# Two packed arrays for the small constants, an earlier load of image 1, and a weight conversion in two halves

## The chip, the cores and the metric

The kernel runs on one core of a Trainium2 chip. The metric is the device time of one launch in microseconds, the median of several runs. The program is one long sequence of instructions on five engines, which are named here as the profile names them: PE multiplies matrices (PEld loads its weights), DVE is the vector engine, ACT the activation engine, POOL the general-purpose engine, SP the engine that issues most of the transfers. [...]

## The reference

Two layers are applied one after the other to x, 32 images of 256 channels by 32 x 32 pixels. Both begin with a group normalisation, and both add their result to their input:

```
x = x + conv(gn(x), weight, bias)      # layer 0
x = x + involution(gn(x), w1, bn, w2, b2)  # layer 1
gn(v):   (v - mean) / sqrt(var + eps) over groups of 8 channels and all pixels
conv:    3 x 3, 256 -> 256 channels; inputs, weights and result rounded to a 16-bit
         float format and clipped at 65504
involution: y = relu(batchnorm(w1 @ v)); k = w2 @ y + b2, a 7 x 7 kernel for each
         pixel and each of 16 groups of channels; out = that kernel on v around the pixel
```

The constants of layer 1 besides w2 and b2 are the four vectors of the batch norm and w1; layer 0 has its weights and its bias.

## The kernel before, in words

**Stages.** One step n of the main loop (line 552) issues a small slice of the work of up to three images at once. `front` (line 289) is a generator that issues the first half of an image's work in slices: sums (add_up, line 221), mean (243), sums of squares (247), variance (252), 1/sqrt (259), scale and offset (263), the normalised input xq (apply, line 283), the convolution (line 337) in four units of 18 matmuls, of which nine use the first half of the weights and nine the second. For each unit DVE clips the result (line 351) and adds it with the bias to x (line 353), and ACT adds x up for layer 1 (line 224). Then come layer 1's normalisation into xn, the product with w1 (line 385), and transposes (line 400). The per-pixel kernels (line 415), their move to memory (`scatter`, line 469), their reload as bands (`load_bands`, line 482) and the involution's matmuls (`sums`, line 504) follow later in the loop. Each image takes 16 steps; image 1 enters `front` 16 steps after image 0.

**Order.** Everything inside `with tc.manual_schedule()` (line 550) keeps the order in which it is written on each engine. What stands ahead of it, lines 126 to 201, is placed between these instructions by the planner of the framework, as its own estimate of when inputs arrive suggests. The chain of small instructions from the batch norm's constants (lines 182 to 188) is such a case: on DVE it was put behind line 353 of image 0's first unit, and between the instructions of the second.

**Group normalisation.** `group` (line 228) takes per-partition sums, transposes them on DVE, adds eight of them, and transposes back. It is called for the mean and again for the variance, so each normalisation goes ACT, DVE, ACT, DVE, ACT several times.

**The start.** SP issues the two halves of image 0, the two halves of the convolution's weights (line 161, into the space of the later bands), w2 in two pieces (165), b2 in fourteen (170), the bias (173), w1 (175), the four vectors of the batch norm in two pieces each (180), and three writes of zeros to the borders of the memory for the per-pixel kernels (201). Behind these stand the loads of images 1 to 3, which the loop asks for at line 591, 63 steps ahead of an image's involution (LOAD). `quantize_weights` (line 203) clips and converts the weights to 16 bits on DVE, both halves one after the other, at step FRONT + 2: in DVE's queue that is after image 0's mean and ahead of its variance. POOL then fills the two bands and the ring w_sb with zeros.

Of the kernel before, what the change touches and what calls it, by code (L numbers as in the profile page):

```python
# [9 lines left out]
F32 = mybir.dt.float32  # L10
AF = mybir.ActivationFunctionType
ALU = mybir.AluOpType

P = 128
# [4 lines left out]
CH = C // P  # L19
K0, PAD0 = 3, 1  # L20
K1, PAD1 = 7, 3
TAPS = K1 * K1
CR = 64
G = 16
# [5 lines left out]
F16_MAX = 65504.0  # L30
# [21 lines left out]
V = 2  # L52
A = G // V
# [3 lines left out]
SW = K1 * G  # L57
S = H + 2 * PAD1
T = 4
TW = P // T  # L60
# [6 lines left out]
NPIX = 6  # L67
RING = 32
SCRATCH = 4096
FRONT = -56  # L70
LOAD = -63
LEAD = 18
# [3 lines left out]
def tile_quant_conv_then_involution(  # L76
# [1 line left out]
    tc: tile.TileContext,  # L78
    x: bass.AP,
    w0: bass.AP,  # L80
    bias0: bass.AP,
    w1: bass.AP,
    bn_gamma: bass.AP,
    bn_beta: bass.AP,
    bn_mean: bass.AP,
    bn_var: bass.AP,
    w2: bass.AP,
    b2: bass.AP,
    out: bass.AP,
):  # L90

# [1 line left out]
    nc = tc.nc  # L93
    PSUM = bass.MemoryType.PSUM

    const = ctx.enter_context(tc.tile_pool(name="const", bufs=1))
# [9 lines left out]
    def load_x(b):  # L106
        xt = xpool.tile([P, CH, N], F32, tag="x", name=f"x_{b}")
        for h in range(CH):
            nc.sync.dma_start(xt[:, h], x[b, h * P : (h + 1) * P])
        return xt  # L110
# [15 lines left out]
    x_tiles = {0: load_x(0)}  # L126
# [18 lines left out]
    bands = [const.tile([P, SIDES, WINC * WB + PAD], F32, name=f"band_{i}") for i in range(NBAND)]  # L145
# [7 lines left out]
    w_sb = const.tile([P, 2, RING, A, WIN, V], F32, name="w_sb")  # L153
# [3 lines left out]
    wq = const.tile([P, CH, K0 * K0, C], F16, name="wq")  # L157
    staged = []
    for kh in range(CH):
        wf = bands[kh].rearrange("p d n -> p (d n)")[:, : K0 * K0 * C].rearrange("p (k c) -> p k c", c=C)  # L160
        nc.sync.dma_start(wf, w0[kh * P : (kh + 1) * P])
        staged.append(wf)
    w2_sb = const.tile([P, K1, SW], F32, name="w2_sb")
    for i in range(2):
        nc.sync.dma_start(w2_sb[i * CR : (i + 1) * CR], w2)
    b2_sb = const.tile([P, 2, 2, SW], F32, name="b2_sb")
    for dj in range(K1):
        t, e = divmod(dj, 2)
        for r in range(2):
            nc.sync.dma_start(b2_sb[t * TW : (t + 1) * TW, e, r], b2[dj].partition_broadcast(TW))  # L170

    bias_sb = const.tile([P, CH], F32, name="bias_sb")
    nc.sync.dma_start(bias_sb, bias0.rearrange("(h p) -> p h", p=P))
    w1_sb = const.tile([P, CH, CR], F32, name="w1_sb")
    nc.sync.dma_start(w1_sb, w1.rearrange("(h p) o -> p h o", p=P))

    bn = const.tile([P, 4], F32, name="bn")
    for i, v in enumerate((bn_gamma, bn_beta, bn_mean, bn_var)):
        for r in range(2):
            nc.sync.dma_start(bn[r * CR : (r + 1) * CR, i : i + 1], v.unsqueeze(1))  # L180
    bn_ve = const.tile([P, 1], F32, name="bn_ve")
    nc.vector.tensor_scalar(bn_ve, bn[:, 3:4], BN_EPS, None, ALU.add)  # L182
    bn_r = rsqrt(bn_ve, [P, 1], "bn")
# [16 lines left out]
        )  # L200
        nc.sync.dma_start(to, bands[NBAND - 1][:H, 0, :n].unsqueeze(1).to_broadcast([H, cols, n]))

    def quantize_weights():

        for kh in range(CH):
            nc.vector.tensor_scalar(wq[:, kh], staged[kh], F16_MAX, -F16_MAX, ALU.min, ALU.max)
            nc.gpsimd.memset(bands[kh], 0.0)
        nc.gpsimd.memset(w_sb, 0.0)

    class GroupNorm:  # L210

# [195 lines left out]
    def weights(b, r0):  # L407

        pws = [ps_w.tile([P, 2, 2, SW], F32, tag=f"pw{i}", name=f"pw{i}") for i in range(2)]
        for r in range(2):  # L410
            for t in range(T):
                for i in range(2):
                    half = slice(i * CR, (i + 1) * CR)
                    dj = slice(2 * t, min(2 * t + 2, K1))
                    nc.tensor.matmul(  # L415
                        pws[i][t * TW : (t + 1) * TW, : dj.stop - dj.start, r],
                        y_sb[b % 2][half, (r0 // 2 + r) * W : (r0 // 2 + r + 1) * W],
                        w2_sb[half, dj],
                        start=True,
                        stop=True,  # L420
                    )
        for i in range(2):
            for e in range(2):
                p = P if e == 0 else (K1 // 2) * TW
                for r, rows, d0, d1, at in ring_pieces(b, r0 + 2 * i):
                    evict(pws[i][:p, e, r : r + rows], e, r, rows, d0, d1, at)
# [42 lines left out]
    def scatter(b, k, part):  # L469

        at = (b * H + k * TR) % RING
        for dj in range(part, K1, 2):
            t, e = divmod(dj, 2)
            to = bass.AP(
                tensor=wd.tensor,
                offset=wd.offset + k * TR * ROW + dj * WPIX + (K1 - 1 - dj) * WB,
                ap=[[WPIX, TW], [ROW, TR], [1, WB]],
            )
            rows = w_sb[t * TW : (t + 1) * TW, e, at : at + TR]
            nc.sync.dma_start(to, rows.rearrange("p s a r v -> p s (a r v)"))  # L480
# [23 lines left out]
    def sums(b, m):  # L504

        k, d = divmod(m, SIDES)
        j0 = 0 if d else PAD1
        band = bands[(b * K + k) % NBAND][:, d]
        px = pixels[(b * K + k) % NPIX][:, d]
        for h in range(CH):  # L510
            for v in range(2):
                for g, at, top, f, l in windows(b, m):
                    p = slice(g * KP, (g + 1) * KP)
                    of = band[p, V * g * XR + j0 * WB : V * g * XR + (j0 + WINI) * WB]
                    of = of.rearrange("p (j a r v) -> p j a r v", a=A, r=WIN, v=V)
                    for t in range(T):
                        a = h * T + t
                        nc.tensor.matmul(  # L518
                            at[t * TW : (t + 1) * TW, h, :, f - top : l - top],
                            px[p, a, v * GC : v * GC + TW],  # L520
                            of[:, :, a, f - top : l - top, v],
                            start=(h, v) == (0, 0),
                            stop=(h, v) == (CH - 1, 1),
                        )

    def add_windows(b, m):

        d = m % SIDES
        to = x_tiles[b].rearrange("p h (r c) -> p h r c", c=W)
        j0 = d * (JC - PAD1)  # L530
        for g, at, top, f, l in windows(b, m):
            x_at = to[:, :, f:l, j0 : j0 + WINI]
            of = at.rearrange("p h j r -> p h r j")[:, :, f - top : l - top]
            nc.vector.tensor_tensor(x_at, of, x_at, ALU.add)  # L534

    def store(b, k):

        cols = slice(k * NT, (k + 1) * NT)
        nc.sync.dma_start(out[b].rearrange("(h p) n -> p h n", p=P)[:, :, cols], x_tiles[b][:, :, cols])
# [5 lines left out]
    def due(n, lag):  # L545

        b, i = divmod(n - lag, per)
        return (b, i) if 0 <= b < B else (None, None)

    with tc.manual_schedule():  # L550
        fronts = {}
        for n in range(FRONT, B * per + 2):
            b, i = due(n, FRONT)
            if i == 0:
                fronts[b] = front(b)
            later = list(fronts)
            for part in range(2):
                for b in list(later):
                    got = next(fronts[b], fronts)
                    if got is fronts:  # L560
                        fronts.pop(b)
                    if got is not LATER:
                        later.remove(b)
            if n == FRONT + CH:
                quantize_weights()
            b, i = due(n, 0)
            if b is not None and i % 2 == 0:
                sums(b, i // 2)
            b, i = due(n, 1)
            if b is not None and i % 2 == 0:  # L570
                add_windows(b, i // 2)
                if i // 2 == M - 1:
                    store(b, 1)
                    x_tiles.pop(b)

            b, i = due(n, 2)
            if b is not None and i == 2 * (M - 1 - SIDES):
                store(b, 0)
            b, i = due(n, -LEAD)
            if b is not None and i % 2 == 0:  # L580
                weights(b, i // 2 * WR)

            for part in range(2):
                b, i = due(n, -LEAD + 1 + part)
                if b is not None and i % 2 == 0:
                    for k in range(K):
                        if i // 2 == min((k + 1) * TR // WR, H // WR - 1):
                            scatter(b, k, part)
            b, i = due(n, LOAD)
            if i == 0 and b > 0:  # L590
                x_tiles[b] = load_x(b)

            b, i = due(n, 3 - 4 * NBAND)
            if b is not None and i % 4 == 0:
                load_bands(b, i // 4)
# [37 lines left out]
```

## Time and profile before

| | |
|---|---|
| median of three runs | 1375.84 us |
| the three runs | 1378.53, 1371.69, 1375.84 us |
| the profiled execution | 1370.77 us, of which its span is 1368.9 us |
| busy share of the span | PE 92%, POOL 74%, DVE 60%, ACT 53% |
| mean granted clock of PE | 0.988 |
| first matmul of image 0's convolution | 18.06 us after the start |
| first matmul of image 1's convolution | 40.63 us |
| first matmul of the involution (line 518) | 93.62 us |

A line of the timeline has the start in microseconds, the duration, the engine, the line of the kernel, the operation, the tile written and the tile read, shape and count; in brackets stands how long the engine had been idle and what ended it. Adjacent instructions of one kind are put together, so that the duration of such a line can contain waits. An SPq line tells of SP's queue: the time it takes to issue a transfer, not that of the transfer. A row of the table of windows has the stretch, its length, the busy time of an engine with the number of instructions, the granted clock of PE (1.00 is full speed), the busy share of the transfer engines, and the rate.

### The profile page before, as it was taken

The numbers are of one execution on the slowest core, as the hardware profiler recorded it, in microseconds if no ns is written. First come the engines' busy times: TensorE is split into PE (matmuls) and PEld (weight loads), VectorE is DVE, ScalarE is ACT, GpSimd is POOL, SyncE is SP. The second block draws the span as 40 slices with busy tenths as digits, with TensorE's granted clock in tenths as the row PEclk, the third lists the DMA queues.
The fourth block names the chain that finished last, engine by engine and source line by source line (L and its number), as shares of the span: only waits on it lengthen the run. The fifth ranks groups of instructions, "written<-read, shape, count | busy, mean of one in ns | idle before, by whom it ended". The sixth has DMA issues, their size and how long they took to land.

```text
span 1368.9 us, 69378 instructions
## 1 busy us (share of the span) xinstructions
PE 1261.3 (92%) x29440; PEld 805.5 (59%) x29440; DVE 820.2 (60%) x2539; ACT 726.8 (53%) x1699; POOL 1012.1 (74%) x1818
## 2 busy tenths in 40 slices
PE   4799999999999999999999999999999999999664
PEld 2356666656665665666666566556656656666543
DVE  3366566666666666665666666656666666666542
ACT  4866565465655555665555565545555555553300
POOL 9057777778777777877777777777777777778875
PEclk9999999999999999999999999999999999999997
DMA  6089999999999999999999999999999999999995
GB/s 218 6 221 289 278 283 290 296 274 287 277 285 284 279 287 282 291 290 282 289 286 285 276 279 282 280 294 269 282 290 278 286 285 287 289 287 268 275 273 170
DMA packets 366563, 369.93 MB, mean 270 GB/s; under 512 B 78960, under 2 KB 308528, under 8 KB 366000
## 3 DMA queue, kind: packets, MB, share of 16 engines
q1 hardware_dynamic: 280240, 235.90, 58.0%
q0 software_dynamic: 86016, 129.60, 34.1%
q8 instruction: 234, 3.83, 1.2%
q14 instruction: 73, 0.60, 0.1%
HBM read 184.43 MB, written 180.76 MB: 267 GB/s over the span
## 4 chain that ended last, share of the span: by engine, by line
PE 72%; DMA 13%; issue 4%; POOL 3%; ACT 3%; SPq 2%; DVE 2%; POOLq 0%; DVEq 0%; ACTq 0%
PE pc L337 29%; PE acc L518 23%; PE pw L415 13%; DMA band<-wd 7%; PE py L385 4%; DMA wd<-w_sb 4%; PE pt L400 3%; POOL band L493 3%; ACT junk L224 1%; SPq L480 1%; DMA x<-in_x 1%; DMA out<-x 1%; DVE w_sb L439 1%; DMA w_sb<-in_w 1%; SPq L493 0%
## 5 line engine op out<-in xcount | busy, mean ns | idle before, releaser
L493 POOL DMA_DIRECT2D band<-wd x1792 | 978.0, 548 | 343.2 <-DMA band<-wd 209.9
L439 DVE TENSOR_TENSOR w_sb<-pw,b_sb 128x224 f32<-128x224 f32 (+7 forms) x1280 | 331.4, 324 | 434.7 <-PE pw L415 428.7
L337 PE MATMUL pc<-xq,wq 128*128 128x496 f16 (+3 forms) x2304 | 534.5, 378 | 30.6 <-ACT xq L283 24.3
L518 PE MATMUL acc<-band,pixels 64*32 64x190 f32 (+1 forms) x16384 | 428.5, 329 | 50.5 <-DMA band<-wd 28.0
L337 PEld LDWEIGHTS <-wq 128*128 128x128 f16 x2304 | 206.5, 98 | 324.3 <-issue 110.9
L518 PEld LDWEIGHTS acc<-band,pixels 64*32 64x32 f32 x16384 | 300.8, 106 | 141.8 <-issue 89.4
L415 PE MATMUL pw<-w_sb,y 64*32 64x224 f32 (+1 forms) x8192 | 290.6, 330 | 17.7 <-issue 16.8
L534 DVE TENSOR_TENSOR x<-acc,x 128x380 f32<-128x380 f32 (+1 forms) x512 | 262.3, 512 | 32.9 <-PE acc L518 24.0
L415 PEld LDWEIGHTS pw<-w_sb,y 64*32 64x32 f32 x8192 | 186.1, 105 | 48.3 <-issue 33.4
L404 ACT COPY pixels<-pt 128x512 f32<-128x512 f32 x128 | 73.7, 576 | 237.2 <-PE pt L400 237.2
L224 ACT ACTIVATE junk<-x 128x512 f16<-128x512 f32 (+1 forms) x192 | 146.4, 763 | 16.6 <-DVE bn_ve L182 6.0
L224 ACT ACTIVATE junk<-x,mean 128x1024 f16<-128x1024 f32 x128 | 147.1, 1149 | 4.3
L255 ACT ACTIVATE s<-back,eps 128x2 f32<-128x2 f32 x64 | 19.0, 296 | 198.6 <-DVE back L240 198.5
L351 DVE TENSOR_SCALAR q<-pc 128x512 f16<-128x512 f32 x128 | 87.1, 680 | 18.2 <-PE pc L337 18.1
L283 ACT ACTIVATE xn<-x,off,rstd 128x512 f32<-128x512 f32 x128 | 96.2, 800 | 0.0
L353 DVE SCALAR_TENSOR_TENSOR x<-q,bias_sb,x 128x512 f32<-128x512 f16 x128 | 94.6, 739 | 0.3
L400 PEld LDWEIGHTS pt<-ident,xn 128*128 128x128 f32 x512 | 63.3, 141 | 26.6 <-issue 2.7
L400 PE MATMUL pt<-ident,xn 128*128 128x128 f32 x512 | 77.3, 274 | 0.8 <-ACT pixels L404 0.7
L283 ACT ACTIVATE xq<-x,off,rstd 128x1024 f16<-128x1024 f32 x64 | 75.8, 1227 | 1.0 <-PE pc L337 0.9
L385 PEld LDWEIGHTS py<-xn,w_sb 128*64 128x64 f32 x2048 | 62.8, 138 | 16.8 <-issue 6.7
L385 PE MATMUL py<-xn,w_sb 128*64 128x64 f32 x2048 | 67.7, 224 | 2.8 <-ACT xn L283 2.2
L245 ACT ACTIVATE mean<-back 128x2 f32<-128x2 f32 x64 | 12.6, 196 | 101.2 <-DVE back L240 101.2
(40 smaller groups left out, 372.7 us busy)
## 6 DMA issues: line engine op xcount, KB each, us to landing
wd<-w_sb SPq DMA_DIRECT2D x896, 160.0 KB
band<-wd POOLq DMA_DIRECT2D x1792, 70.5 KB, 4.9
x<-in_x SPq DMA_DIRECT2D x64, 512.0 KB
out<-x SPq DMA_DIRECT2D x64, 512.0 KB
band<-wd SPq DMA_DIRECT2D x256, 70.5 KB
band<-in_w SPq DMA_DIRECT2D x2, 1152.0 KB
w_sb<-in_w SPq DMA_DIRECT2D x2, 196.0 KB
wd<-band SPq DMA_DIRECT2D x2, 180.0 KB
```

The lines of the kernel that those rows point to most:

```text
L224: nc.scalar.activation(junk[:, n0:n1], src[:, h, n0:n1], func, bias=bias, accum_out=self.sums[:, i : i + 1])
L283: nc.scalar.activation(dst, src, AF.Identity, bias=self.off[:, one], scale=self.rstd[:, one])
L337: nc.tensor.matmul(pc.rearrange("p (r c) -> p r c", c=W)[:, r0 - nt * RT : r1 - nt * RT, c0:c1], wq[:, kh, k, mh * P : (mh + 1) * P], xq[: ...
L351: nc.vector.tensor_scalar(q, pc, F16_MAX, -F16_MAX, ALU.min, ALU.max)
L353: nc.vector.scalar_tensor_tensor(xt[:, mh, cols], q, bias_sb[:, mh : mh + 1], xt[:, mh, cols], ALU.add, ALU.add)
L385: nc.tensor.matmul(py[i * CR : (i + 1) * CR, cols], w1_sb[:, kh, :], px[:, r : r + 2], start=kh == 0, stop=kh == CH - 1,)
L400: nc.tensor.transpose(pt[:, i, h * P : (h + 1) * P], xn[:, h, (m + i) * P : (m + i + 1) * P], ident)
L415: nc.tensor.matmul(pws[i][t * TW : (t + 1) * TW, : dj.stop - dj.start, r], y_sb[b % 2][half, (r0 // 2 + r) * W : (r0 // 2 + r + 1) * W], w ...
L439: nc.vector.tensor_tensor(to, of[:, :, d0:d1], bias[:, :, d0:d1], ALU.add)
L493: queue.dma_start(band[j::JC, :, j * WB : j * WB + WPIX], src)
L518: nc.tensor.matmul(at[t * TW : (t + 1) * TW, h, :, f - top : l - top], px[p, a, v * GC : v * GC + TW], of[:, :, a, f - top : l - top, v], ...
L534: nc.vector.tensor_tensor(x_at, of, x_at, ALU.add)
```

## The change

The host packs the bias, the four vectors of the batch norm and w1 into one array of 128 rows (`early`, 134 numbers a row) and w2 and b2, already repeated as the tiles need them, into another (`late`, 1232 numbers a row). The kernel loads each in one transfer and takes the tiles as views. The load of image 1 is asked for between the two; the loop loads images from 2 on. `quantize_weights` does one half of the weights a call: the first at step FRONT + 2 as before, the second four steps later, which puts it behind image 0's variance and reciprocal in DVE's queue.

```diff
+EARLY = CH + 4 + CH * CR
+LATE = K1 * SW + 2 * 2 * SW
...
-    w2_sb = const.tile([P, K1, SW], F32, name="w2_sb")
-    for i in range(2):
-        nc.sync.dma_start(w2_sb[i * CR : (i + 1) * CR], w2)
-    b2_sb = const.tile([P, 2, 2, SW], F32, name="b2_sb")
-    for dj in range(K1):
-        t, e = divmod(dj, 2)
-        for r in range(2):
-            nc.sync.dma_start(b2_sb[t * TW : (t + 1) * TW, e, r], b2[dj].partition_broadcast(TW))
-
-    bias_sb = const.tile([P, CH], F32, name="bias_sb")
-    nc.sync.dma_start(bias_sb, bias0.rearrange("(h p) -> p h", p=P))
-    w1_sb = const.tile([P, CH, CR], F32, name="w1_sb")
-    nc.sync.dma_start(w1_sb, w1.rearrange("(h p) o -> p h o", p=P))
-
-    bn = const.tile([P, 4], F32, name="bn")
-    for i, v in enumerate((bn_gamma, bn_beta, bn_mean, bn_var)):
-        for r in range(2):
-            nc.sync.dma_start(bn[r * CR : (r + 1) * CR, i : i + 1], v.unsqueeze(1))
+    early_sb = const.tile([P, EARLY], F32, name="early_sb")
+    nc.sync.dma_start(early_sb, early)
+    bias_sb = early_sb[:, :CH]
+    bn = early_sb[:, CH : CH + 4]
+    w1_sb = early_sb[:, CH + 4 :].rearrange("p (h o) -> p h o", h=CH)
+    x_tiles[1] = load_x(1)
+    late_sb = const.tile([P, LATE], F32, name="late_sb")
+    nc.sync.dma_start(late_sb, late)
+    w2_sb = late_sb[:, : K1 * SW].rearrange("p (k n) -> p k n", n=SW)
+    b2_sb = late_sb[:, K1 * SW :].rearrange("p (e r n) -> p e r n", r=2, n=SW)
...
-    def quantize_weights():
-
-        for kh in range(CH):
-            nc.vector.tensor_scalar(wq[:, kh], staged[kh], F16_MAX, -F16_MAX, ALU.min, ALU.max)
-            nc.gpsimd.memset(bands[kh], 0.0)
-        nc.gpsimd.memset(w_sb, 0.0)
+    def quantize_weights(kh):
+
+        nc.vector.tensor_scalar(wq[:, kh], staged[kh], F16_MAX, -F16_MAX, ALU.min, ALU.max)
+        nc.gpsimd.memset(bands[kh], 0.0)
+        if kh == CH - 1:
+            nc.gpsimd.memset(w_sb, 0.0)
...
-            if n == FRONT + CH:
-                quantize_weights()
+            if n in (FRONT + CH, FRONT + CH + 4):
+                quantize_weights((n - FRONT - CH) // 4)
...
-            if i == 0 and b > 0:
+            if i == 0 and b > 1:
                 x_tiles[b] = load_x(b)
```

## The prediction

> **What bounds the kernel now.** I read the page first, then the chain of waits up to 90 us, then the timelines of DVE, PE and SP from 0 to 60 us, and last the table of windows for PE's clock.
>
> ```profile
> PE 1261.3 (92%) x29440; PEld 805.5 (59%) x29440; DVE 820.2 (60%) x2539; ACT 726.8 (53%) x1699; POOL 1012.1 (74%) x1818
> PE   4799999999999999999999999999999999999664
> ```
>
> PE is the bound of the body: 90% or more in all slices but the first two and the last three. The diff touches only what runs in the first 35 us, so all there is to win lies in the first slices (34 us each), in the time in which PE is idle or slow. Three places are left: PE starts at 18.06, it idles from 34.87 to 40.63, and after that it runs at half speed.
>
> ```profile
> 11.71 1.81 DVE L206 TENSOR_SCALAR wq<-band 128x2304 f16<-128x2304 f32 x1 [1.44 <-DMA band<-in_w]
> 13.45 0.19 DVE L234 STREAM_TRANSPOSE across<-sums 128x32 f32<-128x32 f32 x1
> 14.14 0.29 ACT L255 ACTIVATE s<-back,eps 128x2 f32<-128x2 f32 x1 [3.58 <-DVE back L240]
> 18.06 16.80 PE L337 MATMUL pc<-xq,wq 128*128 128x512 f16 x72 [18.06 <-ACT xq L283]
> 24.53 3.65 SPq L109 DMA_DIRECT2D x<-in_x  x6
> 24.93 0.15 DVE L182 TENSOR_SCALAR bn_ve<-bn 128x1 f32<-128x1 f32 x1
> 29.43 1.06 ACT L224 ACTIVATE junk<-x 128x1024 f16<-128x1024 f32 x1 [3.51 <-DMA x<-in_x]
> 36.25 0.30 ACT L255 ACTIVATE s<-back,eps 128x2 f32<-128x2 f32 x1 [0.82 <-DVE back L240]
> 39.35 2.36 ACT L283 ACTIVATE xq<-x,off,rstd 128x1024 f16<-128x1024 f32 x2
> 40.63 6.03 PE L337 MATMUL pc<-xq,wq 128*128 128x512 f16 x18 [5.76 <-ACT xq L283]
> 47.44 3.97 PE L337 MATMUL pc<-xq,wq 128*128 128x512 f16 x18 [0.78 <-DVE q L351]
> ```
>
> Image 0's variance (13.45) stands behind the second weight conversion, which waits for its transfer; ACT had nothing to do for 3.58 us. Image 1's load is issued at 24.53, its data land at 29.35, and ACT waits 3.51 us for them.
>
> ```profile
> 37.50:38.00 0.50, 0.00 (x0) 1.00 0.00 0
> 38.00:38.50 0.50, 0.00 (x0) 0.51 0.00 0
> 44.50:45.00 0.50, 0.50 (x3) 0.67 0.00 0
> 45.00:46.00 1.00, 1.00 (x6) 1.00 0.00 0
> ```
>
> The clock (the number after the count) falls to half at 38.0 and is back at 44.83. So the 18 matmuls at 40.63 take 6.03 us where those at 47.44 take 3.97.
>
> [...] 38.0 to 44.83 is two times 3.41, and the falls and rises after 1300 us (1311.2, 1314.6, 1324.8, 1328.2) lie on the same grid. It goes further: a 2.58 us gap (1307.21 to 1309.79) was enough to halve the clock and one of 2.23 (1290.44 to 1292.67) was not; by the grid, a window falls when PE was busy for less than about 41% of it, that is idle for over 2.0 us. [...] of the weights' 256 packets the last falls between 10 and 11 us and most of w2 comes after them, but the first piece of b2 slipped ahead.
>
> **The change, part by part.**
>
> *Transfers.* 26 small transfers leave SP's queue, which spends 2.60 to 22.45 on them (6.6 of that waiting for earlier ones), and two come in at about 0.45 each. Image 1's pair is issued at about 3 to 4 instead of 24.53. In ring order it lands behind x of image 0, the weights and `early`: the second weights' landing (11.65) plus 1.12 MB at 0.43 MB/us, 14.3. If all that SP issues after it (`late` 0.63 MB, images 2 and 3 2.1 MB) shares the engines evenly, 6.3 later, 20.6. ACT needs it at 23.0 (below), so it is hidden either way. The border writes now meet POOL's fill of the third band, over at 7.7; images 2 and 3 may wait behind that, and are first read at 51.9, so nothing. `late` (w2) lands by 21 at the worst and is first used at 60.9 before. POOL's fills keep their rate: the first two bands 14.15 to 26.04 behind its fill of pixels, later than both conversions in either kernel; the ring until 34.6, first written after 61. Nothing.
>
> *Second conversion moved.* Its 1.8 us leave the path. The squares of image 0 end on ACT at 10.57, the first conversion at 10.28, so the variance begins at 10.62 instead of 13.45: **2.83** earlier. With what follows unchanged (13.45 to 18.06 is 4.61) PE starts at 15.23. The second conversion goes behind the reciprocal (11.8), where its data are in (11.65): 11.85 to 13.65. PE needs that half after nine cold matmuls of 0.43, at 19.1; DVE is free until 20.6. If image 1 and `late` shared the transfer engines with it, it would land 1.75 MB / 0.43 = 4.1 later and end at 17.6: still covered. The first half has no cover: each microsecond that it lands after 8.5 costs one beyond the first 0.3. Nothing new is ahead of it; I take 0, and 1.0 as the upper end.
>
> *Batch norm's chain.* It has ten small instructions, nine on DVE at 0.14 to 0.16 and a root on ACT. Its place is chosen by the planner, and the trace of before can't show the new one. Behind the second conversion it is free (DVE idles from 13.65 to 20.6). Ahead of the variance DVE waits for `early`, which lands at about 11.65 + 0.2: 1.2 us of the 2.83 go. One of them between variance and reciprocal costs 0.2. Below nothing is excluded: DVE was not late behind it before. I take 0, with 1.2 as the end.
>
> *Image 1 no longer late.* Image 0's first unit is added up on ACT until 23.0 (25.84 - 2.83), image 1's sums take 2.39 and end at 25.4, the mean follows the second unit at 26.7, and the squares end at 29.5. What is late next? DVE's queue holds image 1's variance behind the third unit of image 0. PE finishes that at 31.07 - 2.83 = 28.24 (the units take 3.81 each, the last ends at 34.87). From the end of a unit to line 255 it took 2.14 (46.66 to 48.80), from line 255 to line 283 3.10 (36.25 to 39.35), from there to the matmul 1.28. So image 1's convolution starts at 28.24 + 6.52 = 34.76 and not 40.63: **5.87** earlier, of which 2.83 is the earlier start and 3.04 the smaller gap: PE ends image 0 at 32.04 and idles 2.72 instead of 5.76.
>
> *Clock.* Before lost 6.03 - 3.97 = 2.06. A gap of 2.72 escapes only if a grid boundary splits it into two parts under 2.0 each: (2.0 - 0.72) / 3.41 = 37%. Otherwise the clock is low for one window of 3.41, 0 to 0.7 of it in the gap, which costs 1.4 to 1.7. I take 1.65, a gain of 0.4; the other end is 2.06.
>
> *Sum.* 5.87 + 0.4 = 6.3; less 0.1 for the small instructions of the batch norm that may stand on the path, **6.2**. After 46 us the waits are all relative (ACT and PE alternate on the chain up to 90 us, PE alone after), so this stays. From the profiled 1370.77 (span 1368.9 and 1.87 around it) that gives 1364.6. This execution is 5.1 below the median of the runs; the four executions known (1370.77, 1371.69, 1375.84, 1378.53) average 1374.2 and lie within 7.8. I start from the 1374.2: **1368.0**.
>
> **The rivals.**
> - *The clock stays up.* 2.06 in place of 0.4: 7.9, so 1366.3. For it: two more gaps of about 2 us that it survived; against it: the 2.58.
> - *The batch norm's chain goes ahead of the variance.* 5.0: 1369.2. For it: the planner puts it where it thinks that its data are in, and these now come third. Against it: before, it stood where the real data landed, so the planner's idea of landings isn't far off.
> - *It goes ahead of image 0's mean: slower.* DVE would stand from 7.0 until `early` lands at L, with the mean, squares and variance behind it. PE then starts at L + 0.2 + 8.2 (18.06 - 2.83 - 7.04) and image 1's convolution at L + 27.9; with the 0.4 of clock it is slower from L = 13.1. In ring order L is 11.8 (1.3 faster); if `early` shares the engines with image 1 and `late` it is 15.7: 2.6 slower, 1376.8. For it: b2's first piece shows that order can be broken; but that let a small one go first.
> - *The gain is given back.* The transfer engines are 92% busy over the span (58.0 and 34.1), and a stage that they pace could take the 6 us. Then 1373.5. Against it: up to 180 us no wait for a transfer stands on PE's chain; waits for bands appear from 1290 on.
>
> **How the numbers follow.** Likeliest 0.42, clock up 0.20, chain ahead of the variance 0.22, ahead of the mean 0.08, given back 0.08. A median of a few runs with a spread of 7.8 blurs each by about 3. The first three with that reach from 1363 to 1372; the other two, 0.16, lie beyond 1373. Range 1363.0 to 1374.5. About 0.5% (6.9 us) is what a measurement of this kernel can tell from no change; from the median of the runs that bound is 1369.0. Below it fall about 60% of the likeliest case, 75% of the second and 45% of the third: faster 0.50; same 0.45; slower 0.05, from the spread alone, as no case reaches +6.9.
>
> **What would show it.** First matmul at 15.2, image 1's at 34.8 and its first 18 matmuls in 4.0 or 5.6; the second conversion behind line 261; ACT not waiting for image 1; the batch norm's chain between 13 and 21 on DVE. The start wrong: line 234 at 12 or later behind line 182 or 206. The sum wrong: image 1's convolution 6 earlier and the involution's first matmul (93.62) not earlier by as much.

## The result, and the profile after

Over twelve runs each, the changed kernel takes 1371.58 us in the median (1363.8 to 1378.67) and the kernel before 1380.26 (1371.69 to 1388.19). The ratio is 0.9935 with a 95% interval of 0.9909 to 0.9961: 9.0 us faster, between 5.4 and 12.6. The kernel before had 1375.84 in its first three runs; its later ones were slower. The profiled execution of the changed kernel took 1367.45 us, its span is 1365.7.

The page's first part and its slices, after. PE's share is the same. Besides slices at the two ends, one digit differs from before: an 8 for a 9 in the 34th slice.

```profile
PE 1262.2 (92%) x29440; PEld 808.8 (59%) x29440; DVE 819.5 (60%) x2539; ACT 725.7 (53%) x1699; POOL 1012.0 (74%) x1818
PE   4999999999999999999999999999999998999675
```

The timeline of the start, after. Lines are numbered anew: 194 is the weight conversion, 171 the batch norm's first instruction, 244 the variance on ACT, 272 the normalised input, 326 the convolution.

```profile
3.35 0.97 SPq L105 DMA_DIRECT2D x<-in_x  x2
10.72 0.21 DVE L223 STREAM_TRANSPOSE across<-sums 128x32 f32<-128x32 f32 x1 [0.44 <-ACT junk L213]
11.44 0.30 ACT L244 ACTIVATE s<-back,eps 128x2 f32<-128x2 f32 x1 [0.82 <-DVE back L229]
11.85 1.68 DVE L194 TENSOR_SCALAR wq<-band 128x2304 f16<-128x2304 f32 x1
13.45 0.14 DVE L171 TENSOR_SCALAR bn_ve<-early_sb 128x1 f32<-128x1 f32 x1
15.35 16.72 PE L326 MATMUL pc<-xq,wq 128*128 128x512 f16 x72 [15.35 <-ACT xq L272]
23.06 1.06 ACT L213 ACTIVATE junk<-x 128x1024 f16<-128x1024 f32 x1
30.40 0.30 ACT L244 ACTIVATE s<-back,eps 128x2 f32<-128x2 f32 x1 [0.86 <-DVE back L229]
33.51 2.35 ACT L272 ACTIVATE xq<-x,off,rstd 128x1024 f16<-128x1024 f32 x2
34.78 5.66 PE L326 MATMUL pc<-xq,wq 128*128 128x512 f16 x18 [2.71 <-ACT xq L272]
41.22 3.97 PE L326 MATMUL pc<-xq,wq 128*128 128x512 f16 x18 [0.78 <-DVE q L340]
```

The variance stands right behind the squares (10.72, where it was 13.45), the second conversion behind it with its data already there (no wait in brackets), and ACT goes on to image 1 at 23.06 without waiting. PE's gap ahead of image 1 is 2.71 us where it was 5.76.

PE's clock around that gap, after (stretch, length, busy time and count, clock, transfers):

```profile
34.50:35.00 0.50, 0.22 (x2) 1.00 0.04 16
35.00:35.50 0.50, 0.50 (x3) 0.63 0.00 0
38.00:38.50 0.50, 0.50 (x2) 0.50 0.00 0
38.50:39.00 0.50, 0.50 (x4) 0.96 0.00 0
```

It falls at 35.13 and is back at 38.54, one stretch of 3.41 us; the first 18 matmuls take 5.66 and not 3.97. In this trace and in that of before, every later change of the granted clock lies a whole number of steps of 3.41 us behind the first rise (18.06 after, 20.94 before): the fall at 35.13 is five steps behind it, and that at 38.01 in the kernel before is five, too. Such a step is what the prediction calls a window of the grid.

The involution's first matmul comes at 87.41 (93.62 before), 6.21 earlier. Behind it the lead wanders. Read at ACT's activation of each image (line 392 before, 381 after) it is 6.22 for image 0, 3.3 for image 6, 0.7 for image 19, 6.2 for image 25, slightly below nothing for images 26 and 28 (-0.1 and -0.6) and 1.3 for image 31. From image 3 to image 30 an image takes 38 to 43 us in either trace, and once 44.6. So one pair of profiles can't say what is left at the end, and the experiments are read in two ways: the start from the trace, where the order is fixed, and the whole from the ratios over many runs.

### The profile page after: what moved, and what is told of

It reads as the page before. It is cut to its first block, busy times and chain, and to the rows that moved or that the text cites. A ratio compares the mean times of both kernels' runs of the same rounds, so it can differ in the third digit from the quotient of the medians.

```text
span 1365.7 us, 69351 instructions
## 1 busy us (share of the span) xinstructions
PE 1262.2 (92%) x29440; PEld 808.8 (59%) x29440; DVE 819.5 (60%) x2539; ACT 725.7 (53%) x1699; POOL 1012.0 (74%) x1818
## 4 chain that ended last, share of the span: by engine, by line
PE 67%; DMA 19%; issue 4%; POOL 4%; ACT 3%; DVE 2%; SPq 1%; POOLq 0%; DVEq 0%; ACTq 0%
PE pc L326 27%; PE acc L507 21%; DMA band<-wd 14%; PE pw L404 12%; DMA wd<-w_sb 5%; POOL band L482 4%; PE py L374 3%; PE pt L389 3%; ACT junk L213 1%; DVE w_sb L428 1%; SPq L469 1%; ACT xn L272 0%; DMA x<-in_x 0%; SPq L482 0%; ACT xq L272 0%
## 5 line engine op out<-in xcount | busy, mean ns | idle before, releaser
L428 DVE TENSOR_TENSOR w_sb<-pw,late_sb 128x224 f32<-128x224 f32 (+7 forms) x1280 | 331.0, 324 | 437.7 <-PE pw L404 437.6
L404 PE MATMUL pw<-late_sb,y 64*32 64x224 f32 (+1 forms) x8192 | 288.0, 331 | 18.7 <-issue 17.8
L404 PEld LDWEIGHTS pw<-late_sb,y 64*32 64x32 f32 x8192 | 186.2, 106 | 46.7 <-issue 31.9
L213 ACT ACTIVATE junk<-x 128x512 f16<-128x512 f32 (+1 forms) x192 | 146.3, 762 | 14.4 <-DVE x L342 11.9
L342 DVE SCALAR_TENSOR_TENSOR x<-q,early_sb,x 128x512 f32<-128x512 f16 x128 | 94.8, 740 | 0.3
L374 PEld LDWEIGHTS py<-xn,early_sb 128*64 128x64 f32 x2048 | 62.6, 138 | 17.0 <-ACT mean L234 8.1
L374 PE MATMUL py<-xn,early_sb 128*64 128x64 f32 x2048 | 67.5, 224 | 3.1 <-ACT xn L272 2.2
```

The costliest lines, as they stand in the source:

```text
L213: nc.scalar.activation(junk[:, n0:n1], src[:, h, n0:n1], func, bias=bias, accum_out=self.sums[:, i : i + 1])
L342: nc.vector.scalar_tensor_tensor(xt[:, mh, cols], q, bias_sb[:, mh : mh + 1], xt[:, mh, cols], ALU.add, ALU.add)
L374: nc.tensor.matmul(py[i * CR : (i + 1) * CR, cols], w1_sb[:, kh, :], px[:, r : r + 2], start=kh == 0, stop=kh == CH - 1,)
L404: nc.tensor.matmul(pws[i][t * TW : (t + 1) * TW, : dj.stop - dj.start, r], y_sb[b % 2][half, (r0 // 2 + r) * W : (r0 // 2 + r + 1) * W], w ...
L428: nc.vector.tensor_tensor(to, of[:, :, d0:d1], bias[:, :, d0:d1], ALU.add)
```

## The experiments

In this table the start is the involution's first matmul, and the gain at the start is against 93.62. The gain in all is worked out from the ratio, times the median of the kernel before in the same set of runs. Each start is that of one profiled execution.

| kernel | first matmul | image 1's convolution | involution | gain at the start | ratio, 95% interval | gain in all |
|---|---|---|---|---|---|---|
| before | 18.06 | 40.63 | 93.62 | | | |
| changed | 15.35 | 34.78 | 87.41 | 6.2 | 0.9935, 0.9909 to 0.9961 | 9.0 |
| e1 split only | 15.50 | 41.43 | 94.23 | -0.6 | 1.0012, 0.9989 to 1.0035 | -1.7 |
| e2 image 1 third | 18.09 | 37.95 | 90.58 | 3.0 | 0.9963, 0.9937 to 0.9989 | 5.1 |
| e3 packed only | 18.87 | 39.70 | 90.67 | 2.9 | 0.9928, 0.9903 to 0.9953 | 9.9 |
| e4 all but the load | 15.65 | 35.26 | 87.89 | 5.7 | 0.9897, 0.9864 to 0.9930 | 14.2 |
| e5 before, fills later | 18.06 | 40.58 | 93.54 | 0.1 | 1.0001, 0.9976 to 1.0026 | -0.1 |
| e6 changed again | 15.20 | 35.71 | 86.68 | 6.9 | 0.9937, 0.9904 to 0.9969 | 8.7 |
| e7 unpacked | 15.22 | 35.70 | 88.32 | 5.3 | 0.9939, 0.9912 to 0.9965 | 8.4 |
| e8 pulled | 15.23 | 32.2 | 83.99 | 9.6 | 0.9888, 0.9849 to 0.9928 | 15.5 |
| e9 fill first | 15.31 | 36.07 | 87.14 | 6.5 | one run, 1362.45 us | |
| e10 batch norm ahead | 22.74 | 43.28 | 94.25 | -0.6 | one run, 1379.82 us | |
| e11 pulled, warmed | 15.69 | 31.1 | 82.89 | 10.7 | 0.9846, 0.9815 to 0.9878 | 21.3 |
| e12 pulled again | 15.50 | 33.5 | 85.28 | 8.3 | 0.9854, 0.9830 to 0.9879 | 20.2 |

Where image 1's convolution follows without a gap (e8, e11, e12) its start is worked out: the end of the run of 90 matmuls less the 3.97 us of the last 18. The ratios of e1 to e4 are of one set of runs, those of e5 to e8 of a second (medians of the kernel before 1378.27 and 1383.12), those of e11 and e12 of a third (1382.93).

**The conversion alone.**

```diff
-    def quantize_weights():
+    def quantize_weights(kh):
...
-            if n == FRONT + CH:
-                quantize_weights()
+            if n in (FRONT + CH, FRONT + CH + 4):
+                quantize_weights((n - FRONT - CH) // 4)
```

> The kernel before with the weight conversion in two halves and nothing else. My theory, that the gains of the parts are limited by image 1's load: the first matmul at 15.3 us instead of 18.06, but image 1's data still land at 29.35, so that its convolution starts at 40.6 as before, with a gap of 8.5 us on PE instead of 5.76, and the involution's first matmul stays at 93.6, within 0.5. Time as before, ratio 1.000 within 0.003. Rival, that the parts add up: image 1's convolution at 37.8, the involution at 90.8, 2.8 us faster.

The first matmul came 2.6 us earlier, and nothing of it reached image 1. The parts don't add up: alone, this one is worth nothing. But the second conversion went otherwise than I had thought, and image 1's convolution was 0.8 later than before and not level. The timeline of this run, DVE, POOL, PE and ACT:

```profile
13.33 6.81 DVE L205 TENSOR_SCALAR wq<-band 128x2304 f16<-128x2304 f32 x1 [1.25 <-DMA band<-in_w]
12.95 5.97 POOL L206 MEMSET band<- 128x7056 f32 x1
20.20 15.75 PE L337 MATMUL pc<-xq,wq 128*128 128x496 f16 x63 [0.78 <-DVE wq L205]
30.00 0.20 ACT L115 ACTIVATE bn_s<-bn_ve 128x1 f32<-128x1 f32 x1 [3.46 <-DVE bn_ve L182]
30.24 1.06 ACT L224 ACTIVATE junk<-x 128x1024 f16<-128x1024 f32 x1
```

The second conversion took 6.81 us in place of 1.8, beside POOL's fill of the first band (5.97 us), which had begun 0.38 earlier. Its nine cold matmuls done, PE waited 0.78 us for it. Runs e5 and e9 take this up.

Whether this wait is also what made image 1 late is not shown. ACT begins image 1's sums at 30.24, where it began them at 29.43 before, and two things come at that time. On ACT the root of the batch norm's chain stands ahead of the sums at 30.00; in this kernel the chain was put behind image 0's second unit, which PE's wait delays. And SP issued image 1's load at 25.40, 0.87 later than before, as the fourteen pieces of b2 took it 13.48 us and not 12.62; landing as long after its issue as before (29.35 less 24.53), the data would be there at 30.2, an estimate.

**Image 1's load alone.** `x_tiles[1] = load_x(1)` goes ahead of the load of w2, and nothing else changes.

> The kernel before with image 1's load moved ahead of all small constants; those stay in their 26 transfers, and the weights are converted in one go. My theory: first matmul at 18.06 as before, ACT does not wait for image 1, the gap ahead of its convolution is 2.7 us, the convolution starts at 37.6 instead of 40.63, the involution at 90.2 with the 0.4 us of clock: 3.4 us faster, ratio 0.9975. Rival, that the small constants, now 0.9 us later, hold up the first unit's addition: the bias is read at 24.27 before, and all that follows moves by what it is late.

Image 1's convolution moved by 2.7 and the involution by 3.0; 3.4 was expected. The gap was 2.93, all of it in one step of 3.41 us counted from the first rise, and the clock fell at the step's end (38.30). The constants' lateness cost little: the bias, issued at 20.01, was there for line 354 at 24.42 (24.27 before).

**The packing alone.** The two arrays and transfers as in the change, image 1's load left to the loop, the conversion in one go.

> The small constants in two arrays and transfers, image 1's load left to the loop, the weights converted in one go. My theory: SP is free of the 26 issues, so that image 1's load goes out by 13 us at the latest and its data are there well ahead of 25.9, when ACT can use them. So it gives what the third place gives: image 1's convolution at 37.6, the involution at 90.2, ratio 0.9975. Rival, that the place of the load matters: its data come behind the border writes and images 2 and 3 and ACT waits for them; then image 1's convolution is later than 37.6 by that wait.

The involution moved by 2.9 where 3.4 was foreseen, and that it came so near is luck. Image 1's convolution was due at 37.6 and came at 39.70: the first matmul was 0.8 later than before, since the first conversion took 4.48 us beside POOL's fills of the pixels, and the 72 matmuls took 18.13 us with a long cold start. The clock stayed up after the gap, which gave most of that back. The gap itself is as foreseen, 2.71. Image 1's load goes out at 3.62 (first half) and 11.9, and ACT never waits for it. The third place closes the gap as freeing SP's queue does (2.93 in e2). The ratio, 0.9928, says more than the start does: 9.9 us (6.5 to 13.4).

**All but the load's place.** The changed kernel, with image 1's load left to the loop.

> The changed kernel with image 1's load left to the loop (two packed transfers and the conversion in halves stay). My theory: ACT first needs image 1 at 23.06 and finds it there; first matmul 15.35, image 1's convolution 34.8, involution 87.4, all as in the changed kernel; ratio to before as there, 0.9935 within its interval. Rival, that the third place is needed once the first matmul is earlier: ACT waits for image 1 after 23.06, and image 1's convolution is later than 34.8 by that wait.

The start is that of the changed kernel but for 0.5 (the first matmul 0.3 later). The gap is 2.71, as in the changed kernel, and ACT does not wait for image 1. So the load's third place is worth nothing at the start once the constants are packed. The ratio, 0.9897, came out below the expected interval's edge; again more over the whole than at the start.

**POOL's fills out of the way, in the kernel before.** Both fills of bands behind both conversions.

> The kernel before, but POOL fills both bands with zeros only behind both weight conversions, where it filled the first between them. New theory, from the second conversion that took 6.81 us beside POOL's first band fill when only the conversion was split: DVE's conversion and a POOL fill exclude each other, and in executions in which the second weights land after 13 us the kernel before loses up to 6 us to that fill. Then this one shows a second conversion of at most 1.9 us, a first matmul near 18 to 19, and over many executions it is faster than the kernel before by 1 to 3 us, ratio 0.998 to 0.999. Rival: the 6.81 us were waiting for data, and this kernel is as before, 1.000.

No difference is seen. In the profiled execution the second conversion came at 11.82 and took 1.71, ahead of both fills that were moved (14.15, as in the kernel before). So this profile is no test of the theory, and nothing speaks for a frequent loss in the kernel before; the interval, which reaches down to 0.9976, doesn't exclude the 1 to 3 us that were expected. That a fill keeps a conversion out stayed open until e9.

**The changed kernel again.**

> The changed kernel once more, beside the others of this job, for a second profile of its start and a ratio on the same chip. First matmul within 15.2 to 15.7, image 1's convolution within 34.7 to 35.3, ratio 0.9935 within its interval of 0.9909 to 0.9961.

The first matmul is where it should be and the gap is again 2.71, but the clock went otherwise. The timeline of PE in this run:

```profile
15.20 17.81 PE L326 MATMUL pc<-xq,wq 128*128 128x512 f16 x72 [15.20 <-ACT xq L272]
35.71 3.97 PE L326 MATMUL pc<-xq,wq 128*128 128x512 f16 x18 [2.71 <-ACT xq L272]
```

Image 0's 72 matmuls took 1.1 longer, being cold for longer: the first rise of the clock in the trace is at 20.12 and not at 18.06. Up to that rise the column of the clock reads 1.00, and the cold start shows in the pace alone, 0.43 us a matmul where 0.22 is usual later. Image 1's first 18 ran at full speed (5.66 in the other profile). Image 1's convolution is at 35.71, outside the 34.7 to 35.3 that I gave, for that reason.

**The start without the packing.** The bias, then image 1's load, ahead of the other small constants, which stay in 25 transfers; the conversion in halves; fills of bands behind both.

> The changed kernel's start without its packing: image 1's load behind the bias, ahead of the other small constants, which stay in their many transfers; the conversion in halves; POOL fills the bands behind both halves, so that it can't stand in DVE's way. Theory, that only the start matters: first matmul 15.3, image 1's convolution 34.8 to 35.3, involution 87.4 to 88, and the ratio to before is that of the changed kernel in this job within 0.003. Rival, that the packed constants are worth something in the body too (the two kernels with them gained 7 to 8 us more over the whole time than at the start, the two without them nothing clear): the same start, but a ratio higher than the changed kernel's by 0.004.

First matmul and gap are nearly the changed kernel's (15.22, 2.80). Image 1's convolution (35.70) and the involution (88.32) came later than I gave, since the cold start was long (72 matmuls in 17.69) and the clock fell as well. The ratios in one set of runs, 0.9939 and 0.9937, are the same. This speaks for a gain of the start alone. The intervals still allow some 4 us either way.

**Image 1's normalisation earlier.**

```diff
+PULL = 7
...
         gn.finish()
+        if b == 1:
+            yield from stages(PULL)
...
-            if i == 0:
+            if i == 0 and b != 1:
                 fronts[b] = front(b)
+            if n == FRONT + per - PULL:
+                fronts[1] = front(1)
```

> The changed kernel, in which image 1's sums, mean, squares, variance and scale are issued seven steps earlier, into the time in which ACT waits for image 0's first unit (16.5 to 22.2), so that its normalisation isn't behind image 0's third unit in DVE's queue. Theory, that this queue sets the 2.71 us gap: the gap ahead of image 1's convolution falls to 1.3 if ACT must wait for the last matmul of image 0 to write xq, to nearly 0 if it may write the first half earlier; the clock stays up, so that the first 18 matmuls take 4.0 instead of 5.66; the involution starts at 84.3 or 83.0 instead of 87.41, and the ratio to before is 0.002 to 0.003 below the changed kernel's. Rival, that something else is late next (image 1's data at 16.5): ACT waits for them, and image 0's first unit is added later.

The gap is gone: 90 matmuls in one run. ACT took image 1 at 16.31, without waiting for its data.

```profile
15.23 20.97 PE L329 MATMUL pc<-xq,wq 128*128 128x512 f16 x90 [15.23 <-ACT xq L273]
36.98 3.97 PE L329 MATMUL pc<-xq,wq 128*128 128x512 f16 x18 [0.78 <-DVE q L343]
```

So after the change it is the place of image 1's normalisation among image 0's units, on ACT and DVE, that made the rest of the gap. Everything from the sums to the scale was moved here; the part on why the prediction was right asks which of it was late. The involution's start, 83.99, lies between the two that were expected. The ratio is 0.005 below the changed kernel's (e6) where 0.002 to 0.003 was expected, but the two intervals overlap.

**A fill ahead of the second conversion.** In the changed kernel POOL's fills of the pixels' space go behind its other fills.

> The changed kernel, with POOL's six fills of the pixels' space moved behind all its other fills, so that POOL fills the first band right after the first weight conversion, from about 10.3 to 16.2, and the second conversion, due at 11.8, falls into that fill. Theory, that a POOL fill keeps DVE's conversion out while it lasts: the second conversion stands from 11.8 to about 17.5, some 5.6 us, its data being there; image 0's matmuls need it at about 19, so that little else moves. Rival, that the conversion of 6.81 us in the run with only the split waited for data: it takes 1.7 to 1.9 us here, and POOL's fill is not affected either.

The timeline of DVE and POOL:

```profile
11.80 5.77 DVE L192 TENSOR_SCALAR wq<-band 128x2304 f16<-128x2304 f32 x1
10.37 5.98 POOL L193 MEMSET band<- 128x7056 f32 x1 [2.67 <-DVE wq L192]
17.62 5.98 POOL L193 MEMSET band<- 128x7056 f32 x1 [1.27 <-DVE bn_ve L169]
```

The conversion stood for 5.77 us with no wait for data, and ended 1.22 us after the fill, which itself took its usual time (5.98). In e1 the conversion ended 1.22 after the fill, too, so the rival, a wait for data, falls: the 6.81 of e1 was the fill. POOL was idle for 1.27 us ahead of its second fill, which writes over what the conversion reads.

**The batch norm's chain ahead of the mean.** Lines 171 to 177 of the changed kernel become a function, called at step FRONT + 2 ahead of the stages.

> The changed kernel with the batch norm's chain written ahead of image 0's mean in the fixed order, so that DVE must wait there for the first packed array. It measures when that array lands, and is the way in which I had forecast that the change could end slower. Theory (ring order): line 182's successor, the first instruction of the chain, starts at 11.8, the chain with its root on ACT takes 2.6 to 2.9, image 0's mean starts at about 14.6 and not 7.1, the first matmul at 22.9, image 1's convolution at 42.4: 1.8 us later than in the kernel before. Rival, that the packed array shares the transfer engines with image 1 and the second array: it starts at 15.7 and the rest 3.9 us later still. If it lands early, ahead of the weights, the chain costs nothing to speak of.

```profile
12.63 0.15 DVE L176 TENSOR_SCALAR bn_ve<-early_sb 128x1 f32<-128x1 f32 x1 [12.63 <-DMA early_sb<-in_early]
14.48 0.20 DVE L226 STREAM_TRANSPOSE across<-sums 128x32 f32<-128x32 f32 x1
22.74 17.84 PE L329 MATMUL pc<-xq,wq 128*128 128x512 f16 x72 [22.74 <-ACT xq L275]
43.28 3.97 PE L329 MATMUL pc<-xq,wq 128*128 128x512 f16 x18 [2.71 <-ACT xq L275]
```

The packed array lands at 12.6, near the 11.8 worked out for transfers that land in the order of their issue ("ring order" above), far from 15.7. Image 1's convolution is 2.65 later than in the kernel before, where 1.8 was expected: the cold start was long (72 matmuls in 17.84). The involution is 0.6 later, as the clock stayed up. Here, too, the second conversion met a fill, and took 4.41.

**PE's clock up earlier.** The kernel with the normalisation pulled ahead, and eleven matmuls more; they add work that the reference does not need.

```diff
+    def warm_up(count):
+
+        for _ in range(count):
+            nc.tensor.matmul(
+                acc[0][:, 0], wq[:, 0, 0, :P], wq[:, 0, :2].rearrange("p k c -> p (k c)"), start=True, stop=True
+            )
...
+            if n == FRONT + CH:
+                warm_up(11)
```

> The kernel with image 1's normalisation pulled ahead, and eleven matmuls more, on the first half of the converted weights into a PSUM tile that nothing reads, in PE's queue ahead of image 0's convolution, so that PE's clock is up when that starts. They add work that the reference does not need. Theory: the eleven run at half speed or partly at full from 10.3 to at most 15.0; image 0's 72 matmuls take 15.3 to 15.5 us instead of 16.7 to 17.8; the involution starts 1.4 to 2.5 earlier than with the normalisation pulled alone, at 81.5 to 82.6; ratio to before 0.001 to 0.002 lower than that kernel's in this job. Rival, that what follows on ACT and DVE doesn't keep up with a faster PE (image 1's squares stand ahead of the first unit's sums): the involution's start moves by less than the matmuls' time.

> The kernel with image 1's normalisation pulled ahead once more, as the fellow of the one with the warmed clock and for a narrower interval: involution at 84.0 plus or minus 1.2 (the clock's grid at the start), ratio to before 0.989 to 0.992.

The timeline of PE with the eleven:

```profile
11.02 4.88 PE L278 MATMUL acc<-wq 128*128 128x512 f16 x11 [11.02 <-DVE wq L195]
15.69 19.42 PE L336 MATMUL pc<-xq,wq 128*128 128x512 f16 x90
35.89 3.97 PE L336 MATMUL pc<-xq,wq 128*128 128x512 f16 x18 [0.78 <-DVE q L350]
```

The 90 matmuls take 19.42 where they took 20.97 and 21.98 without; the conversion ended late (10.96), so that the eleven held the convolution up by some 0.2. They all ran at half speed, and the clock rose at 16.09, after the first matmul of the convolution. The involution starts at 82.89 against 83.99 (e8) and 85.28 (e12), the earliest of all the kernels, though a little later than the 82.6 that was the latest expected. The ratio, 0.9846, can't be told from its fellow's 0.9854. That ratio is a miss of its own: 0.989 to 0.992 was expected for e12, and its involution is just outside the 85.2 that I had allowed. Both start the involution earlier than the changed kernel. Over the whole it is likely that they are faster, but not shown beyond doubt: 0.9888 stood beside 0.9937, with intervals that overlap, and in the third set the changed kernel did not run.

## Why the prediction was right

**The second conversion.** Right: 2.83 was forecast, the variance began 2.73 earlier, the first matmul 2.71. The claim that the conversion is covered in the worst case held only because its data were in by 11.85. I had counted its landing and not POOL: had they come after 12.95 to 14.15, where the first band's fill begins, the conversion could have stood for some 5 us more, an estimate from e1 (6.81 us less 1.8). The step that set POOL's fills at nothing asked only when they run, not whom they keep out. e9 shows what that can do to the conversion (5.77 us), though PE, which needs it at 19.2, did not have to wait there.

**The gap.** Right in size: image 1's convolution was forecast at 34.76, and came at 34.78, with 2.71 idle where 2.72 was worked out. The gap is the same in e6; that the time fits to 0.02 is partly luck, since a longer cold start put it at 35.71 there. That image 1's data no longer count is shown by e3 and e4, in which the load's place doesn't matter. The reason given for what is late next, the variance behind image 0's third unit in DVE's queue, is only half of it. The changed kernel's timeline of that point:

```profile
29.03 0.75 DVE L342 SCALAR_TENSOR_TENSOR x<-q,early_sb,x 128x512 f32<-128x512 f16 x1
29.36 0.19 ACT L213 ACTIVATION_READ_ACCUMULATOR junk<-x,mean 128x1 f32 x1
29.70 0.20 DVE L223 STREAM_TRANSPOSE across<-sums 128x32 f32<-128x32 f32 x1
```

DVE takes up the variance (29.70) when it is done with the third unit. But ACT ends image 1's squares only at 29.55, and in the kernel before, with DVE idle, the variance followed the squares by 0.10 (35.54 after 35.44). So the third unit costs some 0.05 us, an estimate from these figures, and ACT, where the squares stand behind image 0's earlier units, is as late. The prediction's own figures have this near tie: the squares until 29.5 and 0.81 more to the variance on ACT (36.25 less 35.44) make 30.3, and by the third unit it is 30.38. It named one side only. e8 moved both; no run moved the variance alone.

**The clock.** Forecast to fall in 63% of cases. It fell in the changed kernel's profile and in e2, e4 and e7, and stayed up in e3, e6, e9 and e10, at gaps of 2.71 to 2.93: four of eight. The 2.0 us behind the forecast are read from two steps of the trace of before: PE was idle for 1.97 us of the one from 1290.70, and the clock stayed up, and for 2.02 us of the one from 1307.77, and it fell. All eight gaps fit the 2.0. Counted in steps of 3.41 us from the first rise in each trace, the largest part of the gap in one step is 2.16 to 2.93 us where the clock fell and 1.61 to 1.94 where it stayed up. But the line is not sharp: late in the changed kernel's trace the clock fell after steps with PE idle for 1.85 us (from 1059.13) and 1.92 us (from 1321.96). The loss when it fell was 1.69 in the changed kernel (5.66 less 3.97); 1.65 was taken. What the forecast left out is the other end: the cold start varies as well (72 matmuls in 16.72 and 17.81).

**The batch norm's chain.** It went where it is free, behind the second conversion (13.45). The forecast of its price elsewhere is right in kind: e10, with it ahead of the mean, is slower at the start than the kernel before. The 1.3 faster that the prediction gave for transfers that land in the order of their issue was too kind. I had counted its first instruction and not the rest of the chain, which takes 1.85 us from 12.63 to 14.48.

**The whole.** 6.2 was the sum, 6.21 came at the start, and 9.0 (5.4 to 12.6) in all, an interval that holds the sum. That the start fits to 0.01 is partly luck, since the same kernel had 6.9 in e6. The time of 1368.0 is 3.6 under the median: the 1374.2 that I started from, from four executions, is 6.1 under the 1380.26 that the kernel before has over twelve runs, and the larger gain made up for part of that. That the gain would be given back in the body is refuted by the ratio; the lead of the profiled pair, down to 1.3 at image 31, is that of one execution of each, and the one of the kernel before (1370.77) lies below all twelve of its runs.

**What stays open.** In e3, e4, e11 and e12 the gain in all is above the gain at the start by 7 to 12 us, more than the intervals allow, and in e8 by 5.9, just at the edge of its interval; in e1, e2 and e5 it isn't. All five have the packed arrays, which could mean something in the body. But the unpacked e7 did as well as the changed kernel beside it, and in the changed kernel itself the difference (2.8 and 1.8) is within the intervals. The cause is not settled.

## What to carry to other kernels

Of several waits at a start, work out which is late next after each is taken away: the split alone gave nothing at the start, the load alone 3.0 us, and both together 6.2, as the split counts only once the load is no longer late. The 26 small transfers kept SP busy or waiting until 22.45 and so held image 1's load back; packing them (e3) and moving the load ahead (e2) shortened the gap alike, and doing both brought nothing clear beyond the packing (e4). When a conversion is moved, look at what another engine is filling at that time, not only at whether its data are there: beside a fill of 5.98 us it took 5.77 us, and 1.36 with POOL idle (e9).

## What was not expected of the hardware

A 32-to-16-bit conversion on DVE that began during a fill of a band on POOL did not end before the fill had. A conversion of 128x2304 took 5.77 us (e9), 6.81 us (e1) and 4.41 us (e10) beside a fill of 5.97 or 5.98, and ended 1.21 or 1.22 us after it each time, where it takes 1.3 to 1.4 us with POOL idle (e9, e10) and 1.4 to 2.0 among the short fills of the pixels' space in the other runs but e3. Other instructions of DVE did not stand in e9: the transposes, the sum and the reciprocal of image 0's variance ran inside the same fill (10.66 to 11.87) and took their usual 0.17 to 0.21 us. The fills stood for the conversions, too. Six fills of the pixels' space took 4.13 us with no conversion ending among them (e3) and 6.55 with both conversions among them (the changed kernel): 1.21 for each conversion. In e3 the first conversion stood from 8.52 to 13.00, 4.48 us, and ended 1.21 after the last of the six fills (11.79). What in the hardware makes the two wait for each other is not shown.
